# A decoder layer on one core: some operand sums moved from VectorE to GpSimd, two filler products in each of the first four slots, and the fillers of the last slots kept to one set of PSUM banks

## The chip, the core and the metric

The kernel runs on one core of a Trainium2 chip. The engines go by the names of the profile: PE is TensorE (matmuls), DVE is VectorE, ACT is ScalarE, POOL is GpSimd, SP issues DMAs. The metric is device time in microseconds (us) of one execution. Three runs of the kernel before gave 655.74, 656.04 and 656.16 us: the median is 656.04.

## What is computed

The layer has an input x of 2 batches × 512 tokens × 1024 features, all in float32:

```python
x = x + attention(layernorm(x))      # 32 heads of 32, 8 key/value heads, RoPE, causal
x = x + xattn(layernorm(x), ctx)     # both sides fake-quantised to 0..255, then a 1024x1024 matmul
x = x + ffn(layernorm(x))            # x @ W_org.T + LoRA experts (8 x rank 64), mixed by a softmax
                                     # over the mean token's scores
fake_quant(v) = (clip(round(v / s + z), 0, 255) - z) * s
```

The projections to queries, keys and values have 1536 output columns: 1024 for queries, 256 for keys, 256 for values.

## The kernel before

**Projections by seven products.** A projection of one weight column (a pair of 128-wide blocks; six columns in the order k, 0, 1, v, 2, 3) is a 2 × 2 block product: two halves of the features, and the two batches. It is computed with seven products of sums instead of eight, after Strassen's scheme. One product (`quarter`, L748) is four matmul calls of 128 × 512, each of which shows as two records, so "x8" in a group of records is one product. The products need sums of their operands, which are made in place:

- of the weights of a column c, T1 to T4 (`weight_sums`, L858), each one subtraction of 128 × 512: T1 = low − other_low, T2 = other_high − T1 (in its own tile t2), T3 = other_low := other_high − other_low, T4 = high − T2. All four are on DVE, one after the other in the lane `(1, "T")`. T2 of a column waits until product P6 of the column two before it is done, since they share a tile.
- of x, S3, S2, S1 and S4 (`sums_of_x`, L885), each in four pieces of 128 × 512, on DVE, in the lane `(0, "S")`. S2 lies in a tile named oT; S4 is a12 − S2 and overwrites a12, so it waits until the product that reads the old a12 (of the last first-stage item, `("first", 2)`) is done.

`g_second` (L787) makes, for each column, P6 from S2 and T2 (records "bank<-oT,t"), P5 from S1 and T1, and P3 from S4; `g_third` (L813) makes P7 with T3 and P4 with T4. Every product is added from PSUM into its result by DVE (L743).

**Slots.** Attention goes through 40 slots, `visit(i)` (L2040). Slot i makes four score tiles on PE (L1120) into the four banks of one set of PSUM. DVE takes a row minimum of each (L1132) and ACT the exponentials and their totals (L1147). When a group of slots is complete, ACT takes logarithms and POOL turns the totals into small terms (nine small operations, L1193 to L1201); a DMA transposes them to mT. Four slots later (LAG = 4) the scores are made again the other way round, together with these terms ("weights", L1218 and L1226), ACT takes their exponentials into pt (L1240), POOL masks the diagonal tiles (L1245), and PE multiplies them by v (L1267). So there are 44 visits, the last four without new scores.

**Fillers.** PSUM has eight banks, two sets of four. Two sets change places with each slot: in each visit the new scores go to one and the weights of LAG slots earlier to the other. Between slots, `fill(us)` gives PE other work: the products of the projections at first, then, for batch 0, the output projection (wo), the quantised matmul (q2, q1T) and others. `fill` adds `us` to a credit (RATE_1 = 5.0 us for slots before 24, RATE_2 = 3.6 after) and takes units from a queue while the credit is over half of UNIT = 3.44 us. A filler's bank comes from the list `allowed`: the four banks of the set `new`, or in the last LAG visits of `1 - new`. In the first four slots, where no weights are made, the fills take 1, 2, 1 and 2 products.

**Who sets the order.** The engines run their instructions in the order in which the program was written. A planner (`Clocks`, L119) models each engine's time and a duration for every instruction. Work beside PE stands in lanes of "hops", each with its engine, its inputs and a condition; `dispatch` (L529) writes hops whose inputs are ready by the model, lanes in sorted order. `force` writes a hop at once when the next unit must have it.

**The quantised matmul.** Row sums of the quantised context are needed for a correction: `g_columns` (L1384) multiplies them by a matrix of ones into bank "cs" (one for each half of 512 columns). For batch 0 this is a sum of eight matmuls per half over the eight tiles q2. For batch 1, in the part after the attention, POOL first adds the eight tiles (q2sum, L1377 to L1382, seven additions of 128 × 1024 in f16), and the matmul takes the sum (L1390). `chain_units` (L1890) says what this unit depends on.

After the slots come the products of the rest: the output projection of batch 1, the feed-forward matrix ("worg"), hidden and up of the experts (L1774, L1821, L1857), with the same scheme of seven products, and sums on DVE.

Of the kernel before, what the change touches and what calls it, by code (L numbers as in the profile page):

```python
# [13 lines left out]
ALU = mybir.AluOpType  # L14
AX = mybir.AxisListType

P = 128
# [30 lines left out]

RATE_1, RATE_2 = 5.0, 3.6
EARLY = 24  # L50
# [61 lines left out]
class Clocks:  # L112
# [45 lines left out]
    def add(self, ins):  # L158
# [48 lines left out]
        else:  # L207
# [8 lines left out]
            elif engine == "Pool":  # L216
                us = 0.25 + 0.0008 * many
            elif kind == "CustomDveAnt":
                us = 0.08 + 0.00104 * many
            elif kind == "TensorScalarPtr" and len(ins_) < 2 + 2 and not ins.is_scalar_tensor_tensor:  # L220
                us = 0.12 + 0.00058 * many
            else:
                us = 0.08 + 0.00106 * many
                if kind == "TensorScalarPtr":
                    us += 0.05
                elif kind == "TensorTensor" and self.at["Pool"] > start and not _in_psum(ins_):
                    us += 0.1
# [19 lines left out]
def kernel(  # L247
# [250 lines left out]
    lanes = {}  # L498
    LEAD = 0.6
    LEADS = {"Activation": 5.0, "Pool": 5.0}  # L500

# [113 lines left out]
    def any_may():  # L615
        return any(may_start(key) for key, _ in queue)

    def fill(us):

        credit[0] += us  # L620
        while any_may() and (is_open() or credit[0] > UNIT / 2):
            if not step():
                credit[0] = min(credit[0], UNIT)
                break

# [232 lines left out]
    def weight_sums(c):  # L858
# [5 lines left out]
        def second():  # L864
# [4 lines left out]
            minus_(t2[c], other_high, low)  # L869

        def fourth():
            minus_(high, high, t2[c])

        may = lambda: xn_free[0] > 0 if i == 0 else i == 1 or ("P6", COLUMNS[i - 2]) in done
        lane(
            (1, "T"),
            Hop("DVE", lambda: minus_(low, other_low, low), lambda: [low, other_low], key=("T", c, 1)),
            Hop("DVE", second, lambda: [other_high], may, ("T", c, 2), lambda: [t2[c]]),
            Hop("DVE", lambda: minus_(other_low, other_high, other_low), key=("T", c, 3)),
            Hop("DVE", fourth, key=("T", c, 4)),  # L880
        )
# [3 lines left out]
    def sums_of_x():  # L885
# [6 lines left out]
        def pieces(i, fn, can=None):  # L892
# [11 lines left out]
        )  # L904
        pieces(
            4,
            lambda k: minus_(a12[:, k, :], a12[:, k, :], s2[:, k, :]),
            lambda: ("first", 2) in done,
        )

# [376 lines left out]
    def load_ctx(b, bufs, dst, release):  # L1287
# [72 lines left out]
        if free[0]:  # L1360
            for k in range(1, CTX // P):
                mine = [("q2", b, i) for i, (n_, _) in enumerate(parts) if n_ in (k - 1, k)]
                last = {"key": ("q2sum", b), "made": lambda: [q2sum[b]]} if k == CTX // P - 1 else {}
                lane(
# [19 lines left out]
    def g_columns(b):  # L1384
        corr[b] = const.tile([P, D], F32, tag="corr", name=f"corr{b}")
        for h in range(2):
            cols = slice(h * 512, (h + 1) * 512)
            ps = mm([P, 512], f"cs{b}_{h}")
            if b in q2sum:
                nc.tensor.matmul(ps, onesh, q2sum[b][:, cols], start=True, stop=True)  # L1390
                yield 0.22
# [498 lines left out]
    def chain_units(b, w_keys):  # L1890

        turned = [("q", n) for n in range(B * NC)] + [("k", n, h) for n in range(B) for h in range(2)]
        columns = [("q2sum", b)] if b else [("q2", b, i) for i in range(CTX // P)]
        unit(("cs", b), turned + columns, lambda: g_columns(b))
# [145 lines left out]
    def visit(i):  # L2040
# [20 lines left out]
        hold(max(when_free))  # L2061
        empty([(old, s) for s in range(4)])
        sc, st = sets[new], sets[old]
# [6 lines left out]
        for s in range(4):  # L2070
            if s == 1 and g >= 0:
                empty([(new, 0)])
                pv = take_bank((new, 0))
                attend(g, pv)
# [13 lines left out]
        if g >= 0:  # L2088
            attended_to(g, pv)
        filler[0] = new  # L2090
        last_slots = i + 1 >= n_slots
        allowed[:] = [(1 - new if last_slots else new, s) for s in range(4)]
        dispatch()
        fill(RATE_1 if i < EARLY else RATE_2)
        if finishing is not None:
# [222 lines left out]
```

## Time and profile before

| | |
|---|---|
| median of three runs | 656.04 us |
| profiled execution | 655.19 us |
| its span | 653.5 us |
| PE busy | 631.9 us (97%) |
| DVE busy | 514.5 us (79%) |
| ACT busy | 299.6 us (46%) |
| POOL busy | 128.8 us (20%) |
| granted PE clock | 0.999 of full |

The span is the time from the first to the last instruction in the profile; 1.7 us of the execution lie around it. In a timeline, a line gives start, duration, engine, the source line, the operation and "output<-inputs" by the program's names, and in brackets how long the engine was idle before it and what ended that. In the waits, a line says which group waited for which, the total in us, how many times, and the longest. In a table of windows, each engine has its busy time and number of instructions, followed by the granted clock, the DMA share and GB/s.

### The profile page before, as it was taken

How to read it: one execution, taken by the hardware profiler on the slowest of the kernel's cores; microseconds unless marked ns; L12 is line 12 of the kernel's file. 1: busy time of each engine (PE TensorE's matmuls, PEld its weight loads, DVE VectorE, ACT ScalarE, POOL GpSimd, SP SyncE). 2: the span in 40 equal slices, each digit the busy share in tenths (PEclk: the TensorE clock that was granted, in tenths of full speed). 3: DMA queues.
4: the chain of work that ended last, by engine and by line, in shares of the span. 5: the costliest groups of instructions: out<-in, count | busy, mean ns of one | idle time of the engine just before them, and what ended most of it. 6: DMA issues, size and time to landing. Idle time of an engine off the chain costs nothing. (4 is left out here: it accounts for less than half of the span.)

```text
span 653.5 us, 9247 instructions
## 1 busy us (share of the span) xinstructions
PE 631.9 (97%) x3190; PEld 301.6 (46%) x3190; DVE 514.5 (79%) x1187; ACT 299.6 (46%) x808; POOL 128.8 (20%) x253
## 2 busy tenths in 40 slices
PE   5998999999999999999999999999999999999997
PEld 5753344444444444444444444444345544444443
DVE  5799889888778988888887689998998544553685
ACT  2145576686655768888897433554101100110100
POOL 2100133233313232333233320440110000000000
PEclk9999999999999999999999999999999999999999
DMA  9930000002021230120101146591000002000105
GB/s 290 335 83 2 9 9 10 10 1 73 10 73 65 73 106 10 46 101 34 33 2 25 25 134 237 169 314 32 1 1 0 33 31 97 1 0 1 65 0 193
DMA packets 42478, 44.64 MB, mean 68 GB/s; under 512 B 19264, under 2 KB 32576, under 8 KB 42432
## 3 DMA queue, kind: packets, MB, share of 16 engines
q1 hardware_dynamic: 24992, 38.82, 17.4%
q10 hardware_dynamic: 17440, 5.25, 4.2%
q8 instruction: 25, 0.41, 0.2%
q14 instruction: 21, 0.17, 0.1%
HBM read 35.66 MB, written 4.19 MB: 61 GB/s over the span
## 5 line engine op out<-in xcount | busy, mean ns | idle before, releaser
L1147 ACT ACTIVATE ms<-ms,stats 128x512 f32<-128x512 f32 (+3 forms) x256 | 141.0, 558 | 70.1 <-DVE stats L1132 70.1
L1132 DVE CUSTOM_DVE_ANT_0 ms<-bank,mask 128x512 f32<-128x512 f32 (+3 forms) x256 | 108.5, 487 | 14.7 <-PE bank L1120 12.9
L1240 ACT ACTIVATE pt<-bank 128x512 f32<-128x512 f32 x160 | 88.0, 590 | 25.3 <-PE bank L1267 9.0
L751 PE MATMUL bank<-xT,wq 128*128 128x512 f32 x192 | 88.0, 600 | 2.7 <-DVE stats L1132 2.7
L1245 POOL TENSOR_SCALAR_AFFINE_SELECT pt<-pt 128x512 f32<-128x512 f32 x64 | 48.9, 782 | 94.5 <-ACT pt L1240 90.3
L1411 PE MATMUL bank<-wo,oT 128*128 128x512 f32 x128 | 59.1, 604 | 0.7 <-ACT pt L1240 0.7
L751 PEld LDWEIGHTS bank<-xT,wq 128*128 128x128 f32 x192 | 34.7, 190 | 41.3 <-issue 35.7
L1218 PE MATMUL bank<-qT,kT 32*128 32x128 f32 (+3 forms) x512 | 49.3, 439 | 1.3 <-DVE x L1420 0.6
L1147 ACT ACTIVATION_READ_ACCUMULATOR ms<-ms,stats 128x1 f32 x256 | 50.1, 196 | 0.0
L1120 PE MATMUL bank<-kT,qT 32*128 32x128 f32 (+3 forms) x512 | 49.0, 461 | 0.0
L1120 PEld LDWEIGHTS bank<-kT,qT 32*128 32x128 f32 x512 | 24.2, 183 | 34.9 <-ACT pt L1240 10.5
L1267 PE MATMUL bank<-pt,v 128*32 128x128 f32 (+3 forms) x512 | 37.8, 435 | 0.0
L1411 PEld LDWEIGHTS bank<-wo,oT 128*128 128x128 f32 x128 | 23.1, 189 | 26.8 <-issue 24.2
L1193 POOL TENSOR_TENSOR stats<-stats,log 128x16 f32<-128x16 f32 x16 | 6.5, 409 | 142.7 <-ACT log L1184 100.3
L1218 PEld LDWEIGHTS bank<-qT,kT 32*128 32x128 f32 x512 | 25.6, 185 | 14.6 <-issue 7.8
L1795 DVE TENSOR_TENSOR x<-x,bank 128x512 f32<-128x512 f32 x36 | 23.1, 680 | 11.1 <-PE bank L1774 5.7
L1411 PE MATMUL bank<-q,q1T 128*128 128x512 bf16 x128 | 28.6, 379 | 1.6 <-ACT pt L1240 1.6
L1267 PEld LDWEIGHTS bank<-pt,v 128*32 128x32 f32 x512 | 16.4, 109 | 27.7 <-issue 24.8
L1774 PE MATMUL bank<-worg,S 128*128 128x512 f32 x64 | 28.3, 592 | 0.0
L1774 PE MATMUL bank<-worg,x3T 128*128 128x512 f32 x64 | 28.0, 594 | 0.0
L1774 PE MATMUL bank<-tb,S 128*128 128x512 f32 x64 | 27.9, 593 | 0.0
L743 DVE TENSOR_TENSOR qT<-bank,qT 128x512 f32<-128x512 f32 x28 | 18.9, 686 | 9.6 <-PE bank L751 9.5
(226 smaller groups left out, 1021.4 us busy)
## 6 DMA issues: line engine op xcount, KB each, us to landing
wq<-in_wqT_dram SPq DMA_DIRECT2D x8, 512.0 KB, 8.5
ctx_raw<-in_ctx_dram SPq DMA_DIRECT2D x8, 512.0 KB, 3.2
wo<-in_woT_dram SPq DMA_DIRECT2D x8, 512.0 KB, 3.1
raw<-in_ctx_dram SPq DMA_DIRECT2D x8, 512.0 KB, 3.9
worg<-in_worgT_dram SPq DMA_DIRECT2D x8, 512.0 KB, 6.2
out_dram<-x SPq DMA_DIRECT2D x16, 256.0 KB, 2.1
x<-in_x_dram SPq DMA_DIRECT2D x7, 512.0 KB, 6.7
x_raw<-in_x_dram SPq DMA_DIRECT2D x4, 512.0 KB, 7.4
```

The costliest lines, as they stand in the source:

```text
L743: nc.vector.tensor_tensor(dst, ps, other, ALU.add)
L751: nc.tensor.matmul(ps[:, part], weight[:, k, :], xs_[:, k, part], start=(k == 0), stop=(k == n - 1),)
L1120: nc.tensor.matmul(sc[s][:, part], qTs[b, c][row(s), t * P : (t + 1) * P], kTs[b][row(s), c // 4, : (t + 1) * P], start=True, stop=True,)
L1132: nc.vector.tensor_tensor_reduce(out=of[s][:, part], in0=sc[s][:, part], in1=mask[:, S - (t + 1) * P :], scale=-scale, scalar=BIG, op0=ALU ...
L1147: nc.scalar.activation(ms[:, part], ms[:, part], AF.Exp, bias=stats[g][:, t, s, 0:1], scale=-1.0, accum_out=stats[g][:, t, s, 1:2],)
L1218: nc.tensor.matmul(sc[s][:, part], kTs[b][row(s), c // 4, kb * P : (kb + 1) * P], qTs[b, c][row(s), kb * P :], start=True, stop=False,)
L1240: nc.scalar.activation(pt[:, s, :], sc[s][:, :n], AF.Exp, scale=scale)
L1245: nc.gpsimd.affine_select(out=diagonal, in_=diagonal, compare_op=ALU.is_ge, fill=0.0, base=0, pattern=[[0, 4], [1, P]], channel_multiplier=-1,
L1267: nc.tensor.matmul(pv[row(s), kb * P :], vs[b][:, kb, h * HD : (h + 1) * HD], pt[:, s, part], start=(kb == 0), stop=(kb == NT - 1),)
L1411: nc.tensor.matmul(ps, l[:, t * P : (t + 1) * P], r[:, cols], start=(k == 0), stop=(k == many - 1))
L1774: nc.tensor.matmul(ps[i], l[:, k, i * P : (i + 1) * P], r(k), start=(k == 0), stop=(k == n - 1))
L1795: nc.vector.tensor_tensor(xh, xh, src, ALU.add)
```

## The change

- T3 and T4 of each column go from DVE to POOL (GpSimd), in a lane of their own, `(1, "T34")`; T1 and T2 stay. T2 of a column now also waits for T4 of the column two before it.
- S4's four pieces go from DVE to POOL, in a lane `(1, "S4")`.
- In the first four slots a fill tops the credit up to two units, and `allowed` holds both sets; once less than one and a half units of credit are left, it is cut back to the set `filler[0]`. Visits up to LAG empty both sets.
- `filler[0]` is changed only in slots with new scores, and `allowed` is the set `1 - new` only after the last of these. So in the last four visits the weights go to the same set each time, and the fillers and the attention product (now from `mm`) to the other.
- POOL adds seven instead of eight tiles into q2sum (six additions); the eighth goes into the bank by a second matmul of each half. The unit's dependences for batch 1 are all q2 tiles and q2sum.
- RATE_1 is 4.7 instead of 5.0, the planner's duration of a two-input operation on POOL is 0.1 + 0.0021 n us, and a fill that finds no step to make calls `dispatch` with a lead of 2.5 us.

```diff
-RATE_1, RATE_2 = 5.0, 3.6
+RATE_1, RATE_2 = 4.7, 3.6
...
-                us = 0.25 + 0.0008 * many
+                us = 0.1 + 0.0021 * many if kind == "TensorTensor" else 0.25 + 0.0008 * many
...
         while any_may() and (is_open() or credit[0] > UNIT / 2):
+            if len(allowed) > 4 and credit[0] < 1.5 * UNIT and not is_open():
+                allowed[:] = [p for p in allowed if p[0] == filler[0]]
             if not step():
                 credit[0] = min(credit[0], UNIT)
+                dispatch(IDLE)
                 break
...
+        def third():
+            nc.gpsimd.tensor_tensor(other_low, other_high, other_low, ALU.subtract)
+
         def fourth():
-            minus_(high, high, t2[c])
-
-        may = lambda: xn_free[0] > 0 if i == 0 else i == 1 or ("P6", COLUMNS[i - 2]) in done
+            nc.gpsimd.tensor_tensor(high, high, t2[c], ALU.subtract)
+
+        def may():
+            if i < 2:
+                return i == 1 or xn_free[0] > 0
+            return ("P6", COLUMNS[i - 2]) in done and ("T", COLUMNS[i - 2], 4) in done
+
         lane(
             (1, "T"),
             Hop("DVE", lambda: minus_(low, other_low, low), lambda: [low, other_low], key=("T", c, 1)),
             Hop("DVE", second, lambda: [other_high], may, ("T", c, 2), lambda: [t2[c]]),
-            Hop("DVE", lambda: minus_(other_low, other_high, other_low), key=("T", c, 3)),
-            Hop("DVE", fourth, key=("T", c, 4)),
+        )
+        lane(
+            (1, "T34"),
+            Hop("Pool", third, tuple, lambda: ("T", c, 1) in done, key=("T", c, 3)),
+            Hop("Pool", fourth, lambda: [t2[c]], lambda: ("T", c, 2) in done, key=("T", c, 4)),
         )
...
-        pieces(
-            4,
-            lambda k: minus_(a12[:, k, :], a12[:, k, :], s2[:, k, :]),
-            lambda: ("first", 2) in done,
-        )
+        for k in range(n):
+            last = {"key": ("S", 4)} if k == n - 1 else {}
+            lane(
+                (1, "S4"),
+                Hop(
+                    "Pool",
+                    lambda k=k: nc.gpsimd.tensor_tensor(a12[:, k, :], a12[:, k, :], s2[:, k, :], ALU.subtract),
+                    tuple,
+                    lambda: ("first", 2) in done and ("S", 2) in done,
+                    **last,
+                ),
+            )
...
-            for k in range(1, CTX // P):
+            for k in range(1, CTX // P - 1):
                 mine = [("q2", b, i) for i, (n_, _) in enumerate(parts) if n_ in (k - 1, k)]
-                last = {"key": ("q2sum", b), "made": lambda: [q2sum[b]]} if k == CTX // P - 1 else {}
+                last = {"key": ("q2sum", b), "made": lambda: [q2sum[b]]} if k == CTX // P - 2 else {}
...
             if b in q2sum:
-                nc.tensor.matmul(ps, onesh, q2sum[b][:, cols], start=True, stop=True)
+                nc.tensor.matmul(ps, onesh, q2sum[b][:, cols], start=True, stop=False)
+                yield 0.22
+                nc.tensor.matmul(
+                    ps, onesb, q2_of(b, CTX // P - 1)[:, cols], start=False, stop=True
+                )
                 yield 0.22
...
-        columns = [("q2sum", b)] if b else [("q2", b, i) for i in range(CTX // P)]
+        columns = [("q2", b, i) for i in range(CTX // P)] + ([("q2sum", b)] if b else [])
...
-        empty([(old, s) for s in range(4)])
+        empty([(old, s) for s in range(4)] + [(new, s) for s in range(4) if i <= LAG])
...
             if s == 1 and g >= 0:
-                empty([(new, 0)])
-                pv = take_bank((new, 0))
+                pv = take_bank((new, 0)) if i < n_slots else mm([P, S], f"pv{g}")
...
-        filler[0] = new
-        last_slots = i + 1 >= n_slots
-        allowed[:] = [(1 - new if last_slots else new, s) for s in range(4)]
+        if i < n_slots:
+            filler[0] = new
+        allowed[:] = [(1 - new if i + 1 == n_slots else new, s) for s in range(4)]
+        if i < LAG:
+            allowed.extend((old, s) for s in range(4))
         dispatch()
-        fill(RATE_1 if i < EARLY else RATE_2)
+        fill(2 * UNIT - credit[0] if i < LAG else RATE_1 if i < EARLY else RATE_2)
```

More of the change, by code (lines that the diff above doesn't have):

```diff
@@ L499 @@
     LEAD = 0.6
+    IDLE = 2.5
     LEADS = {"Activation": 5.0, "Pool": 5.0}
```

## The prediction

> **What bounds the kernel now.** First the shares: PE is busy 631.9 of 653.5 us (97%) at a granted clock of 0.999, DVE 79%, ACT 46%, POOL 20%. So the end is set by how much PE work there is and by PE's gaps, and the gaps are few enough to be listed. The waits of the PE engine, which sum the idle time in front of its groups by what ended it, come second:
>
> ```profile
> PE bank L473 <- DVE xn_a L465: 7.3, 1, 7.3
> PE bank L751 <- DVE stats L1132: 3.6, 4, 1.0
> PE bank L1411 <- ACT pt L1240: 2.3, 3, 0.9
> PE bank L1390 <- POOL q2sum L1382: 1.3, 1, 1.3
> PE bank L473 <- ACT pt L1240: 0.8, 1, 0.8
> ```
>
> The first line is the start of the kernel. The other four, 3.57 + 2.27 + 1.26 + 0.80 = 7.90 us, are places the diff touches. The timeline of PE shows the late ones; the first two lines are of slots 2 and 3, the last of the second context correction:
>
> ```profile
> 62.67 3.70 PE L751 MATMUL bank<-xT,wq 128*128 128x512 f32 x8 [0.96 <-DVE stats L1132]
> 68.32 3.70 PE L751 MATMUL bank<-oT,t 128*128 128x512 f32 x8 [0.88 <-DVE stats L1132]
> ...
> 358.01 1.89 PE L1411 MATMUL bank<-q,q1T 128*128 128x512 bf16 x8 [0.71 <-ACT pt L1240]
> 360.79 1.89 PE L1411 MATMUL bank<-q,q1T 128*128 128x512 bf16 x8 [0.89 <-ACT pt L1240]
> 364.64 3.70 PE L1411 MATMUL bank<-wo,oT 128*128 128x512 f32 x8 [0.67 <-ACT pt L1240]
> 378.51 1.14 PE L473 MATMUL bank<-ident,xn_c 128*128 128x128 f32 x8 [0.80 <-ACT pt L1240]
> ...
> 467.67 0.59 PE L1390 MATMUL bank<-q2sum,onesh 128*128 128x512 f16 x2 [1.26 <-POOL q2sum L1382]
> ```
>
> In each of the first four slots the filler product goes to a PSUM bank whose scores DVE is still reading for their minima (0.77, 0.96, 0.96 and 0.88 us). In the last four slots fillers go to the set that ACT's exponentials still read. At 467.67 two matmuls wait for the last of seven adds on POOL. Third, the windows by stage (PE, PEld, DVE, ACT, POOL busy):
>
> ```profile
> 45.80:77.00 31.20, 27.63 (x121) 11.92 (x124) 27.45 (x76) 15.69 (x52) 2.62 (x9) 1.00 0.02 5
> 77.00:130.00 53.00, 52.90 (x342) 24.38 (x335) 46.93 (x136) 37.50 (x115) 16.68 (x36) 1.00 0.04 9
> 355.00:385.00 30.00, 26.93 (x207) 12.48 (x209) 20.29 (x37) 14.26 (x31) 11.75 (x21) 1.00 0.11 21
> 385.00:467.00 82.00, 81.41 (x224) 36.88 (x213) 77.55 (x127) 32.44 (x36) 19.46 (x12) 1.00 0.55 174
> ```
>
> In 45.8 to 77 us PE and DVE are equally full; POOL is nearly empty there. From 77 to 130 PE has no gap, with DVE at 89%. From 385 to 467 DVE is at 95% while PE has hardly a gap.
>
> **The change, part by part.** A product here is four matmul calls, eight records of 0.429 us from start to start: 3.43 us.
>
> *1. Two products in each of the first four slots.* Slots 0 to 3 took 1, 2, 1, 2 products, now 2, 2, 2, 2; both PSUM sets are allowed, and the first product of a slot goes to the old set, whose readers are done. PE's amount of work does not change, and the 3.57 us of waits on minima go. What is late next: products come earlier, so their operands are asked for earlier. Slot 2's first product is now P6(k), whose x operand S2 is made on DVE in four pieces of 128x512. The order on DVE puts two pieces ahead of slot 2's minima and two behind:
>
> ```profile
> 61.83 0.42 DVE L1132 CUSTOM_DVE_ANT_0 ms<-bank,mask 128x256 f32<-128x256 f32 x1 [0.47 <-PE bank L1120]
> 64.59 0.69 DVE L644 TENSOR_TENSOR oT<-xT,xT 128x512 f32<-128x512 f32 x1
> ```
>
> These minima take 61.83 to 64.59, 2.76 us. In the changed kernel PE reaches the scores of slot 2 at 60.56 (old start) − 1.73 (two waits gone) + 3.43 (one product more) = 62.26, P6(k) at 62.9, its third piece at 62.9 + 4 × 0.43 = 64.6. DVE begins the minima near 63.2, ends them at 65.95, and the third piece is there at 66.6: a new stall of 2.0 us. It is 0 if DVE takes the pieces ahead of the minima, which the written order excludes, and 3.0 if the minima start a microsecond later. I take 2.0. The fourth piece (67.2) and P5(k)'s operand S1 (a piece each 0.62 us against 0.86 us of matmul) add nothing.
>
> *2. S4 on GpSimd (four subtractions of 128x512, f32).* The trace has no such operation on POOL. The nearest rows are q2sum's 128x1024 additions: 2117 ns at best, 2260 median, 2932 at worst. Half of 2.12 is 1.06 us; below it stands DVE's 0.62 us for the same shape, above it the whole 2.12. I take 1.06, as cost per element is what the rows suggest. The four stand behind slot 2's statistics chain (nine small operations, 3.2 us alone, 4.2 to 4.5 when held up), so from about 70.9: ends at 72.0, 73.05, 74.1, 75.2, while the product that reads them wants 72.8, 73.7, 74.5, 75.4. Price 0 to 0.5 (with 2.12 each: 4), I take 0.2.
>
> The GPSIMD Engine Reference of the Trainium skill (4.1 Engine selection) speaks against this part: two-input elementwise work belongs on VectorE, GpSimd takes about twice as long. By its table for 2048 elements an estimate for one piece is 1.12 us, which makes the last piece 0.25 us later and the sum as much worse; no row of this trace has that shape on POOL.
>
> *3. T3 and T4 of six columns on GpSimd (12 × 128x512).* DVE is freed of 16 × 0.62 = 10 us together with S4, POOL gains 16 × 1.06 = 17 us in the first 130 us, where it has 19 of 84 us busy: room enough. The price is contention, which rows of the last stage show:
>
> ```profile
> 426.83 2.12 POOL L1382 TENSOR_TENSOR q2sum<-q2sum,q 128x1024 f16<-128x1024 f16 x1
> 427.40 1.57 DVE L1440 TENSOR_TENSOR off_b<-off_b,qp_sb 128x1 f32<-128x1 f32 x1
> ```
>
> A DVE operation on one element a row, 0.16 us elsewhere (426.64), takes 1.57 us and ends with POOL's. The same holds for S<-x3T at 436.15 (2.28 us, 1.21 at 464.10). DVE operations with a PSUM operand keep 0.67 to 0.69 us in all twelve overlaps I found, so minima and product additions are not held themselves, only queued behind one that is. Slot 4 is the tight place: its weights need the addition of P6(0), which stands on DVE behind T1 and T2 of column 1, each of which may sit out one POOL operation. Bounds 0.1 and 1.2 us, I take 0.5. In slots 5 to 12 and in the last stage's adds the slack is 0.4 to 0.8 us against holds of up to 1.06: 0 if all hide; 5 if five reach PE; I take 0.6, since PE showed no gap from 77 to 130 although rope operations there already alternate with POOL's selects (one at 89.79 is held from 0.75 to 1.20 us).
>
> The Trainium skill's page SBUF — State Buffer (section SBUF: two separate sides) calls the pair of ports shared by GpSimd and Vector an exclusive lock for a whole instruction, which blocks the other fully. If every POOL sum held DVE for its whole length, the 17 us would cancel the 10 us freed and leave DVE 7 us more; the rows above agree on the blocking, but show it only where DVE's two inputs are both in SBUF.
>
> *4. Last slots keep to the empty set.* Fillers of the last four slots go to the set without exponentials: 3.07 us of waits go. But all weights now go to one set: those of slots 37 and 38 must wait for ACT to read those before. Between the weights of 36 and 37 lie two products, between 37 and 38 only eight transposes (0.87 us) against four exponentials of 0.59 us. Bounds: 0 and 2.36 for the first, 0 and 2.36 − 0.87 = 1.5 for the second. I take 0.7 (the exponentials there start late, behind POOL's selects and the DMA that turns the terms, 2.4 us) and 1.1; for slot 39 nothing, as the last attention product (2.36 us) lies between. Sum 1.8.
>
> *5. q2sum with six adds.* The last tile goes into PE itself: the 1.26 us goes, and two matmuls of 0.215 us come (+0.43). The correction also comes one product (3.43 us) later, so POOL's sixth add, a tile earlier, is covered several times; the wait that takes its place is ACT's last q (ends 465.4), which has 4.4 us of slack. Cost beyond 0.43: nothing, or up to 1.3 if that slack is spent by DVE's 95%.
>
> *6. The rest.* RATE_1, the planner's POOL price and IDLE change only the order written out. From slot 13 to the first context correction PE's order is the same; one SP DMA less is issued and three are reordered, all of rows asked for microseconds ahead (3.1 to 6.2 us to landing, DMA 55% at most): 0.
>
> **Sum.** Off: 3.57 + 3.07 + 1.26 = 7.90. On: 2.0 + 0.2 + 0.5 + 0.6 + 1.8 + 0.43 = 5.53. Net −2.4: the profiled execution's 655.19 becomes 652.8. The median of the runs shown is 0.85 above that execution, so I forecast 653.6.
>
> **Rivals.** (A) The new stalls hide: ACT and DVE shift with PE and only the extra matmuls remain: −7.9 + 0.43 = −7.5, 648.6. For it: POOL is idle in 45.8 to 77; against it: S2's place in DVE's order. (B) Stalls swapped one for one: the dearer values of 1 to 4 with the matmuls (3.0 + 0.5 + 1.2 + 0.8 + 2.0 + 0.43) make 7.9: 656, within 0.2%. (C) Slower: POOL's lock. POOL's 16 sums hold DVE's two-input sums and rope operations, product additions queue behind, and the weights or scores of slots 4 to 12 wait. It decides from 2.4 us more on PE than my 1.1, two or three holds in full; 0.9 us in five more places gives 4.5 − 2.4 = +2.1 on the median, 658.1. For it: DVE 89% there; against: DVE has 10 us less to do. (D) The late rule does not deliver, as the weights pay the fillers' wait in full (2.36 + 1.5 for 3.07): +2.1 on my sum, 655.7.
>
> **How the numbers follow.** Runs of this kernel differ by 0.06%, and 0.2%, 1.3 us, is about what can be told from no change. Forecast 0.45, A 0.14, B and D together 0.19, C 0.22. Faster by over 1.3 us (below 654.7): forecast and A, 0.59; same: B and D, 0.19; slower: C, 0.22. The forecast's own range is 651 to 655; the range for 8 in 10 takes in most of A and the nearer half of C: 649.0 to 658.0.
>
> **What would show it.** Right: no PE wait on the minima in the first four slots; one wait of about 2 us near 64.6 of the product from oT and t on DVE's oT; POOL sums of 1.0 to 1.2 us; waits of the weights on exponentials of about 0.7 and 1.1; no wait on q2sum. Wrong if the POOL sums take 2 us, if PE waits on DVE additions between 77 and 130, or if the tail after 385 gets gaps that it did not have.

## The result, and the profile after

The changed kernel takes 666.75 us, median of five runs (666.42 to 667.26). The kernel before took 656.04 in five runs beside it (655.74 to 658.12). The ratio is 1.0159, with an interval of 1.0143 to 1.0176: slower by 10.7 us where 2.4 us faster was forecast. The profiled execution took 667.26 us with a span of 665.5, against 655.19 and 653.5. So the profile has 12.0 us more to explain.

The waits of PE in the kernel after (which group waited for what, total us, times, longest):

```profile
PE bank L1436 <- DMA q1T<-a_b: 5.3, 1, 5.3
PE bank L755 <- DVE oT L648: 1.7, 1, 1.7
PE bank L1239 <- DVE qT L747: 1.2, 3, 0.6
...
PE bank L1799 <- DVE tb L648: 0.8, 1, 0.8
PE bank L1411 <- POOL q2sum L1403: 0.7, 1, 0.7
```

The waits on the minima (3.57 us) and on the exponentials in front of fillers (3.07 us) are gone, as the change says. The wait of 1.7 us on oT is the forecast one. The line at the top is new: one wait of 5.3 us for a DMA, in a place that the prediction costed at nothing. PE's timeline there, in the kernel after:

```profile
385.77 3.70 PE L1799 MATMUL bank<-wo,oT 128*128 128x512 f32 x8
389.53 3.40 PE L1436 MATMUL bank<-q,q1T 128*128 128x512 bf16 x15
398.24 5.31 PE L1436 MATMUL bank<-q,q1T 128*128 128x512 bf16 x16 [5.31 <-DMA q1T<-a_b]
```

Two things are to be seen. PE has nothing from 392.9 to 398.24. And the second group, with one record more, takes 5.31 us where the first took 3.40. The windows of the kernel after say why (PE, PEld, DVE, ACT, POOL busy; granted clock; DMA share; GB/s):

```profile
386.00:398.00 12.00, 6.87 (x23) 2.78 (x23) 9.63 (x15) 3.18 (x5) 0.55 (x1) 1.00 0.96 300
398.00:401.00 3.00, 2.76 (x7) 1.02 (x8) 0.00 (x0) 0.94 (x1) 0.00 (x0) 0.55 0.30 116
401.00:404.00 3.00, 3.00 (x12) 1.46 (x11) 1.16 (x2) 0.00 (x0) 0.00 (x0) 0.88 0.13 31
```

After the gap the granted clock is 0.55 for three microseconds and 0.88 for the next three: the lost clock costs 3 × 0.45 + 3 × 0.12 = 1.7 us on top of the gap. From 386 to 398 us the 16 DMA engines are 96% busy, so the transfer that PE waits for is not held by an idle queue: other transfers run beside it. What was issued around it, on the SP and ACT queues and on DVE, in the kernel after:

```profile
386.02 1.75 SPq L320 DMA_DIRECT2D x<-in_x_dram  x4
...
386.97 0.69 DVE L1487 TENSOR_SCALAR a_b<-xn_b 128x1024 bf16<-128x1024 f32 x1
...
387.71 1.39 ACTq L1535 DMA_TRANSPOSE q1T<-a_b  x1
387.82 1.27 SPq L1317 DMA_DIRECT2D raw<-in_ctx_dram  x2
```

And the same in the kernel before:

```profile
381.72 1.00 DVE L1462 TENSOR_SCALAR a_b<-xn_b 128x1024 bf16<-128x1024 f32 x1
...
382.76 1.25 ACTq L1510 DMA_TRANSPOSE q1T<-a_b  x1
...
385.65 2.06 SPq L320 DMA_DIRECT2D x<-in_x_dram  x4
```

Before, the DMA that transposes the last quantised row tile (a_b to q1T) was issued 2.9 us ahead of four loads of x, 512 KB each. Now it is issued 1.7 us behind them, because a_b is made at 386.97 instead of 381.72, while PE runs only 0.4 us later at this place (the product of wo starts at 385.77 instead of 385.40). The view of the tile q1T gives the time from issue to landing, first in the kernel before, then in the kernel after:

```profile
DMA to landing us min/median/max: 3.1/3.1/6.4
```

```profile
L1436 PE MATMUL bank<-q,q1T x124: 379/379/634, 334.2 to 502.0; 128*128 128x512 bf16 x124
...
DMA to landing us min/median/max: 3.0/3.1/10.5
```

387.71 + 10.5 = 398.2 is the moment at which PE starts again. (In the first line, 634 ns against a median of 379 is a matmul at the lowered clock.) The 6.4 of the kernel before is another of the eight; its last one before the loads took 3.1.

The Trainium skill's page "DMA: Bandwidth & Descriptors" (section Issuing engines are not separate DMA queues) says that DMAs started by different engines run on the same 16 DMA engines and interleave. This case agrees and gives it a size: 3.1 us for the transposing DMA by itself, 10.5 us beside the 2 MB of x and 1 MB of context that SP had issued around it.

The second new place is slot 12. PE's timeline of the kernel after:

```profile
151.17 2.61 PE L1141 MATMUL bank<-kT,qT 32*128 32x512 f32 x6
154.12 0.69 PE L1141 MATMUL bank<-kT,qT 32*128 32x512 f32 x1 [0.35 <-ACT pt L1261]
```

Scores that take 1.14 us elsewhere are spread over 3.5 us here (the second line is their seventh record of eight, the eighth starts at 154.65) and go bank by bank behind ACT's exponentials. No filler product stands between the weights and the scores of the next slot. The fillers that the program wrote between the scores of one slot and the next, in us by the planner's durations, slot by slot:

```
slot     0   1   2   3   4   5   6   7   8   9  10  11  12   13
before 3.4 6.9 3.4 6.9 6.9 3.4 3.4 6.9 3.4 6.9 3.4 3.9 6.9  3.4
after  6.9 6.9 6.9 6.9 6.9 3.4 3.4 3.4 6.9 3.4 3.9 6.9 0.0 10.3
```

The first four slots take two products more, the following ones use up theirs earlier, and by slot 12 the queue has reached a column whose unit needs two new q tiles (the buffers for query results) while 11 of the 12 are still in use. Nothing may start there; it comes a slot later.

### The profile page after: what moved, and what is told of

Read it like the earlier page. It is cut to its first block, busy times and chain, and to the rows that moved or that the text cites. A ratio compares the mean times of both kernels' runs of the same rounds, so it can differ in the third digit from the quotient of the medians.

```text
span 665.5 us, 9260 instructions
## 1 busy us (share of the span) xinstructions
PE 642.3 (97%) x3186; PEld 305.7 (46%) x3192; DVE 512.5 (77%) x1173; ACT 299.4 (45%) x806; POOL 144.9 (22%) x268
## 4 chain that ended last, share of the span: by engine, by line
PE 78%; DVE 13%; issue 3%; ACT 2%; DMA 2%; POOL 1%; ACTq 0%; SPq 0%; DVEq 0%; POOLq 0%
PE bank L755 20%; PE bank L1799 12%; PE bank L1436 10%; PE bank L1882 7%; PE bank L1846 7%; PE bank L1141 6%; PE bank L1239 5%; PE bank L1288 5%; PE bank L473 2%; DVE ms L1153 2%; DMA q1T<-a_b 2%; PE bank L1247 1%; DVE x L1820 1%; DVE S L648 1%; DVE x L1067 1%
## 5 line engine op out<-in xcount | busy, mean ns | idle before, releaser
L1153 DVE CUSTOM_DVE_ANT_0 ms<-bank,mask 128x512 f32<-128x512 f32 (+3 forms) x256 | 108.4, 486 | 16.8 <-PE bank L1141 13.7
L1266 POOL TENSOR_SCALAR_AFFINE_SELECT pt<-pt 128x512 f32<-128x512 f32 x64 | 47.5, 759 | 76.7 <-ACT pt L1261 73.3
L1239 PE MATMUL bank<-qT,kT 32*128 32x384 f32 (+3 forms) x512 | 56.4, 439 | 2.2 <-DVE qT L747 1.2
L1141 PE MATMUL bank<-kT,qT 32*128 32x128 f32 (+3 forms) x512 | 52.3, 460 | 0.3 <-ACT pt L1261 0.3
L1239 PEld LDWEIGHTS bank<-qT,kT 32*128 32x128 f32 x512 | 29.4, 185 | 16.1 <-issue 6.0
L1436 PE MATMUL bank<-q,q1T 128*128 128x512 bf16 x124 | 30.1, 396 | 5.5 <-DMA q1T<-a_b 5.3
```

The source lines that it names most:

```text
L1141: nc.tensor.matmul(sc[s][:, part], qTs[b, c][row(s), t * P : (t + 1) * P], kTs[b][row(s), c // 4, : (t + 1) * P], start=True, stop=True,)
L1153: nc.vector.tensor_tensor_reduce(out=of[s][:, part], in0=sc[s][:, part], in1=mask[:, S - (t + 1) * P :], scale=-scale, scalar=BIG, op0=ALU ...
L1239: nc.tensor.matmul(sc[s][:, part], kTs[b][row(s), c // 4, kb * P : (kb + 1) * P], qTs[b, c][row(s), kb * P :], start=True, stop=False,)
L1266: nc.gpsimd.affine_select(out=diagonal, in_=diagonal, compare_op=ALU.is_ge, fill=0.0, base=0, pattern=[[0, 4], [1, P]], channel_multiplier=-1,
L1436: nc.tensor.matmul(ps, l[:, t * P : (t + 1) * P], r[:, cols], start=(k == 0), stop=(k == many - 1))
```

## The experiments

Theory A: the loss lies in the written order, at two places that the engines' loads do not show: the DMA near 386 us, which the late rule moved behind the loads, and the empty slot 12. Theory B, the rival C of the prediction: the sums on GpSimd hold VectorE, and PE waits for what queues behind them.

**1. The x loads issued behind the last transposing DMA, in the kernel after.** No instruction of PE, DVE or POOL moves.

```diff
+    force(("A", 0, NT - 1))
     for t in range(NT):
         xi = tail_x([P, D], f"x1_{t}")
-        load_x(xi, NT + t)
+        nc.scalar.dma_start(xi, x[(NT + t) * P : (NT + t + 1) * P, :])
```

> The changed kernel, with one thing moved: the four loads of batch 1's x (2 MB) are issued on ACT's queue right behind the transposing DMA of the last quantised row tile (q1T of tile 3), instead of on SP's queue 1.7 us ahead of it. No instruction of PE, DVE or POOL changes its place. Theory A (collision): the 5.31 us wait of PE at 398.24 is that DMA held to 10.5 us by the loads ahead of it; with 3.1 to 4.5 us it lands before PE asks for it at 392.9, so the 5.3 us go, and with them the 1.5 us that the lowered clock costs behind the gap: 666.75 - 6.8 = 660.0. Theory B (POOL holds DVE, and the loss is in the slots): the wait at 398 is only where lateness from the slots is collected; the time stays at 666 to 667, with the lateness showing at another place.

Measured: 659.82 us (658.94 to 660.44, seven runs), ratio to the kernel before 1.0049 [1.0033, 1.0065]. That is 6.9 us less than the kernel after. The issues on ACT's queue, and the tile's DMA:

```profile
387.90 1.25 ACTq L1535 DMA_TRANSPOSE q1T<-a_b  x1
...
389.24 2.30 ACTq L2171 DMA_DIRECT2D x<-in_x_dram  x4
```

```profile
L1436 PE MATMUL bank<-q,q1T x124: 379/379/389, 334.4 to 494.7; 128*128 128x512 bf16 x124
...
DMA to landing us min/median/max: 3.1/3.1/4.1
```

The transposing DMA starts as late as in the kernel after, but lands in 4.1 us at most, PE does not wait, and no matmul is slow. The wait and the lowered clock, 5.3 + 1.7 = 7.0 us, are the loads' doing.

**2. The late rule undone in the kernel after.**

```diff
-                pv = take_bank((new, 0)) if i < n_slots else mm([P, S], f"pv{g}")
+                empty([(new, 0)])
+                pv = take_bank((new, 0))
...
-        if i < n_slots:
-            filler[0] = new
-        allowed[:] = [(1 - new if i + 1 == n_slots else new, s) for s in range(4)]
+        filler[0] = new
+        last_slots = i + 1 >= n_slots
+        allowed[:] = [(1 - new if last_slots else new, s) for s in range(4)]
```

> The changed kernel, with the rule of the last slots as it was before (the sets change places in the last four visits too, fillers in the set that the exponentials read, the attention product in a bank of its own). Theory A with the late rule as its cause: the order of the last slots is again that of before, the quantising of the last row tile is written ahead of the x loads, and the 6.8 us go, while the four waits on exponentials (3.1 us) take the place of the two waits of the weights (2.3): 666.75 - 6.8 + 0.8 = 660.7. Theory B: nothing that matters is in the last slots, 666 to 668. If the late rule is not what moved the quantising, the wait at 398 stays and the time is 667 to 668.

Measured: 660.92 us (660.69 to 663.46, five runs), 1.0074 [1.0049, 1.0099]. No wait on the DMA (it lands in 3.7 us at most, and is issued at 388.97, ahead of the loads at 391.91). The waits that the late rule had removed are back:

```profile
PE bank L1436 <- ACT pt L1261: 1.9, 2, 1.7
...
PE bank L1799 <- ACT pt L1261: 0.8, 1, 0.8
PE bank L473 <- ACT pt L1261: 0.7, 1, 0.7
```

So it is the late rule that put the DMA behind the loads. It loses 7.0 us there to take away 3.4.

**3. The sums back on VectorE in the kernel after (T3, T4 and S4).** These parts of the change's diff are taken out, and all else stays.

> The changed kernel, with T3, T4 and S4 back on DVE (and the planner's price of GpSimd operations as before). Theory A: the wait at 398 stays if it comes from the late rule; of the rest, the holds of DVE by POOL (1.3 us at slot 9 near 122, 0.6 at slot 4, 0.3 at slot 8) go: 666.75 - 2.2 = 664.5. Theory B: most of the 10.7 us goes, 656 to 658.

Measured: 678.63 us (676.49 to 679.22, four runs), 1.0329 [1.0298, 1.036]. Neither theory had this: 12 us slower than the kernel after, where B said faster. Its waits:

```profile
PE bank L1419 <- DMA q1T<-a_b: 5.5, 1, 5.5
PE bank L1394 <- POOL q2sum L1386: 4.2, 1, 4.2
PE bank L755 <- DVE xT L648: 2.3, 1, 2.3
```

The DMA wait is there as before. S4, back on DVE, comes 2.3 us too late for the two products of slot 3. The correction waits 4.2 us for POOL at a place that the sums do not touch: in the written order one product of worg (3.5 us) stands ahead of it, where the kernel after has two. The clock is the largest item: a mean of 0.985 over 677.0 us lacks 10.2 us of clock, where the kernel after (0.997 of 665.5) lacks about 2. Theory B falls as the account of the loss, since the time does not come back with the sums on DVE. How much the sums alone are worth this run does not say, as most of its 12 us lie in places that they do not touch.

**4. The first slots filled by `RATE_1` again, in the kernel after** (and only one set allowed). As RATE_1 is 4.7 here, the fills take 1, 2, 1 and 1 products, one fewer than in the kernel before.

> The changed kernel, with the fills of the first four slots as before (1, 2, 1, 2 products, new set only). In the changed kernel the stretch 46 to 82 us loses as much time on PE as before (4.5 against 4.2 us): the four waits on minima are replaced by 1.72 us for S2 and 0.6 at slot 4. So undoing it alone is worth between 0 and +1.5 by the stretch itself: 666.5 to 668, if the tail keeps its order. If the tail's order turns on how many products have been made by slot 36, the wait at 398 goes here too: 660 to 661.

Measured: 663.52 us (662.43 to 664.69, four runs), 1.0104 [1.0069, 1.0138]. The waits of PE:

```profile
PE bank L1237 <- ACT pt L1259: 5.8, 2, 3.1
PE bank L753 <- DVE stats L1151: 4.8, 4, 2.0
```

The waits on the minima return, larger than before (as in experiment 6), and slot 12 is filled. But the fillers now run out at the other end: slots 39 and 40 get none, and the weights wait 5.8 us for ACT from 355 us on. The DMA comes early enough here. The first slots have fewer products than in the kernel before, and yet the stock ends earlier: by the written order a product goes ahead of the scores of nearly every slot from 14 on, beyond the credit (`hold`). So this run does not give the price of the two early products alone; experiment 8 does, in the kernel before.

**5. Slot 12 filled, on top of experiment 1.** One product goes from slot 11 to slot 12.

```diff
-        fill(2 * UNIT - credit[0] if i < LAG else RATE_1 if i < EARLY else RATE_2)
+        goal = 2 * UNIT if i < LAG else {11: UNIT, 13: 8.72}.get(i)
+        fill(goal - credit[0] if goal else RATE_1 if i < EARLY else RATE_2)
```

> The kernel of the first experiment (the changed kernel with the x loads behind the transposing DMA), with the fills of two slots set by hand: slot 11 takes one product instead of two, slot 12 one instead of none, slot 13 three as it did. In the changed kernel no product may start after slot 11, since two products run ahead and 11 of 12 q tiles are in use (the next column needs two), so the scores of slot 13 follow the attention product at 151 us directly and wait for ACT at each bank (2.0 us), and the weights behind them lose about 1 us. Theory A (running ahead of the q tiles): 659.8 - 2.0 to 3.0 = 656.8 to 657.8. Rival (those scores wait for ACT, which is late by itself): the wait moves to the next slot, 659 to 660.

Measured: 656.49 us (655.94 to 657.48, ten runs), 1.0003 [0.9992, 1.0013]: 3.3 us less than experiment 1, and the same as the kernel before. PE's timeline where the stall was:

```profile
146.49 3.70 PE L755 MATMUL bank<-xT,wq 128*128 128x512 f32 x8
150.12 1.14 PE L1141 MATMUL bank<-kT,qT 32*128 32x512 f32 x8
```

The scores take 1.14 us again. The two places of theory A together are 10.2 of the 10.7 us.

**6. The sums on GpSimd alone, in the kernel before.**

> The kernel before, with T3, T4 and S4 on GpSimd alone (and the planner's price for them). The sums took 1.26 to 2.18 us each in the changed kernel's profile, not 1.06. Theory B (POOL holds DVE, DVE's queue holds PE): holds of 0.3 to 1.3 us at two or three of the slots 4 to 12, 656 + 2 = 657 to 659. Rival (DVE is relieved of 10 us, and the holds are hidden, as the products come no earlier here): 655 to 656.5.

Measured: 659.51 us (658.23 to 661.51, six runs), 1.0048 [1.0028, 1.0068]. Slower alone: the first wait on the minima grows from 0.77 to 2.0 us (all four: 4.8 instead of 3.6), the weights wait 1.1 us for kT, and in the profiled execution the clock drops for 3.4 us behind the first wait (from 49.3 us). That first wait is theory B at work: T1 and T2 of a column take 1.77 and 1.64 us at 42.09 and 43.89, beside POOL's sums of 41.52 to 46.65, where each takes 0.69 in the kernel before, and the minima behind them begin at 48.66 instead of 47.00. The drop of the clock is not needed for the loss: the three of six executions with a mean clock of 0.999 or 1.0 took 658.2 to 658.7 us.

**7. The late rule alone, in the kernel before.**

> The kernel before, with the rule of the last slots alone. If the rule by itself moves the last quantising behind the x loads, the wait for the transposing DMA comes with it: 656 - 3.1 + 2.3 + 6.8 = 662. If it takes the rule together with the two products that were made earlier (which shift what is left to fill in the last slots), there is no such wait: 656 - 3.1 + 2.3 = 655.2.

Measured: 668.23 us (666.4 to 668.35, four runs), 1.0171 [1.0146, 1.0195]. The one edit costs as much as the whole change:

```profile
PE bank L1390 <- POOL q2sum L1382: 6.1, 1, 6.1
PE bank L1411 <- DMA q1T<-a_b: 4.9, 1, 4.9
```

The transposing DMA is issued at 383.36 us here, 0.1 us *ahead* of the loads of x, and still lands only after 8.9 us. The wait of 6.1 us is new: DVE's rounding of the last two raw tiles is written late, so two POOL additions run one after the other (4.9 us from 473.23) with PE waiting.

**8. Two products in the first slots alone, in the kernel before.**

> The kernel before, with two products in each of the first four slots alone. By the written order slots 12, 40, 41 and 42 get no filler at all, as the products run out of q tiles at 12 and of ready work at the end. Off: 3.57 us of waits on minima. On: 1.7 for S2, 2.3 for S4 behind S1 on DVE, 2 to 3 for slot 12, and in the last three slots the weights wait for the exponentials of the set that they have just filled, 4 to 8 us: 656 + 6 to 11 = 662 to 667. Rival (the fills only change places): 653 to 656.

Measured: 664.57 us (663.27 to 666.16, four runs), 1.0125 [1.01, 1.0149]. Waits of 1.7 us on oT and 2.3 us on xT (S4, still on DVE), the latter with half the clock for 3.4 us behind it, the empty slot 12 (its scores start at 152.89, their last record at 156.38) with half the clock for 6.8 us behind it, and empty slots at the end.

**9. Half of S2 on GpSimd, on top of experiment 5.** The stall of 1.7 us on oT is S2's third piece.

```diff
-        pieces(2, lambda k: minus_(s2[:, k, :], a22[:, k, :], a11[:, k, :]))
+        lane((0, "S"), Hop("DVE", lambda: minus_(s2[:, 0, :], a22[:, 0, :], a11[:, 0, :])))
+        lane((0, "S"), Hop("DVE", lambda: minus_(s2[:, 1, :], a22[:, 1, :], a11[:, 1, :]), key=("S", "2a")))
+        for k in (2, 3):
+            fn = lambda k=k: nc.gpsimd.tensor_tensor(s2[:, k, :], a22[:, k, :], a11[:, k, :], ALU.subtract)
+            lane((0, "S2p"), Hop("Pool", fn, tuple, lambda: ("S", "2a") in done, key=("S", 2) if k == 3 else None))
```

> The kernel of the fifth experiment, with the last two of S2's four pieces on GpSimd instead of DVE, behind DVE's first two. POOL is idle from 47 to 66 us there. The stall of 1.72 us in P6(k) comes, by the prediction's step 1, from those two pieces standing on DVE behind slot 2's minima (they end at 65.60, the third piece at 66.3, PE wants it at 64.6). On POOL they need about 1.27 us each from 61.7, beside minima that read PSUM and aren't held: ready at 63.1 and 64.4. Theory: the 1.72 us go, of which up to 0.3 come back in P5(k), as S1's pieces still follow the minima: 656.5 - 1.5 = 655.0. Rival (DVE is the bound of the stretch from 46 to 82 us, and the wait only moves to the next product or to slot 3's scores): 656.0 to 656.8.

Measured: 657.49 us (656.89 to 657.86, twelve runs), 1.0012 [0.9998, 1.0026]: no gain.

```profile
PE bank L755 <- DVE xT L919: 1.1, 1, 1.1
PE bank L755 <- POOL xT L929: 0.9, 2, 0.6
```

The 1.7 us is gone, and S1 (1.1) and S4 (0.9) wait in its place.

**10. The six additions alone, in the kernel before** (the two matmuls for each half, POOL one tile less).

> The kernel before, with q2sum of seven tiles and the eighth multiplied into the bank by PE, alone. The prediction's step 5: 1.26 us of wait go, 0.43 us of matmul come, 656.0 - 0.8 = 655.2. Rival (the wait is not POOL's last add but the clamp of the last tile on DVE, which is written late, at 463.5, and ACT's rounding behind it, 465.4: PE then waits for the seventh tile's add or for ACT): a wait of 0 to 0.7 stays, 655.2 to 656.2.

Measured: 654.25 us (653.82 to 655.2, twelve runs), 0.9963 [0.9949, 0.9977]. It is the only part that gains, and faster than both kernels. Its timeline at the correction:

```profile
466.52 0.38 PE L1390 MATMUL bank<-q2sum,onesh 128*128 128x512 f16 x1
466.74 0.38 PE L1392 MATMUL bank<-q,onesb 128*128 128x512 bf16 x1
```

No wait stands in front of it. The spans of the two profiles differ by 0.7 us (652.8 and 653.5), the fastest runs by 1.4 (653.82 and 655.21), the ratio says 2.4; the runs of the kernel before reach up to 659.15 beside it. Part of the ratio is theirs: five of the 23 had a mean clock of 0.996 or 0.997 and took 658.15 to 659.15 us, the other 18 average 655.93, which is 1.6 us above the 654.32 of this run's twelve, all at 0.998 or more. The profile accounts for 0.7 us; where the other 0.9 come from stays open.

**11. The x loads later, on top of experiment 7** (the edit of experiment 1).

> The kernel of the seventh experiment (the kernel before with the late rule alone), with the four x loads issued on ACT's queue behind the last transposing DMA, as in the first. There the loads were issued 0.1 us after the transpose (383.46 against 383.36), not 1.7 us ahead of it, and it still took 8.9 us. If the loads' traffic is what holds it, the wait of 4.88 us and about 2.5 us of slower clock behind it go: 668.2 - 7.4 = 660.8. The wait of 6.13 us for q2sum (two of POOL's adds are written late, behind DVE's clamp at 471) and the slower clock behind it stay, as no order changes. Rival (the transpose is slow by itself at that place): 667 to 669.

Measured: 662.6 us (662.05 to 664.92, four runs), 1.0093 [1.0063, 1.0124]: 5.6 us less than experiment 7. PE still waits 3.6 us for q1T, which lands in 7.5 us: two loads of context (SP, 383.44) are issued 0.1 us behind it, and the x loads 1.4 us behind. In experiment 1, where the context was issued 1.7 us ahead and the x loads 1.3 us behind, it was 4.1. So 1 MB right behind the transposing DMA delays it, too. The 6.1 us on q2sum stays.

**12. Six additions, and both sets allowed in the first slots with the old fills** (1, 2, 1, 2), in the kernel before.

> The kernel before with the six adds of the tenth experiment, and with one rule of the changed kernel's first slots: where a fill of slots 0 to 3 has credit for two products (slots 1 and 3, as in the kernel before), the first goes to the old set, whose readers are done. The number of products in these slots stays 1, 2, 1, 2; all sums stay on DVE. Theory (the waits on the minima go, and the operands of P6 and P3 are asked for at most 1.8 us earlier, within what DVE has in hand): 654.3 - 0.96 - 0.88 = 652.4. Rival (DVE is the bound of 46 to 82 us, and each wait taken away there comes back at the next operand, as in the ninth experiment): 654.0 to 655.0.

Measured: 655.12 us (654.71 to 656.34, twelve runs), 0.998 [0.997, 0.9989]: not better than experiment 10.

```profile
PE bank L753 <- DVE stats L1134: 1.7, 2, 1.0
PE bank L1122 <- DVE qT L681: 1.5, 1, 1.5
...
PE bank L753 <- DVE xT L646: 0.6, 1, 0.6
```

Of the 3.6 us of waits on the minima 1.8 go; 1.5 on the queries and 0.6 on S4 come.

## Why the prediction was wrong

The step that failed is *6. The rest*: "RATE_1, the planner's POOL price and IDLE change only the order written out ... three are reordered, all of rows asked for microseconds ahead (3.1 to 6.2 us to landing, DMA 55% at most): 0." The largest price of the change was in the DMAs' order, and it came from the late rule, whose step (4) looked at PE and ACT alone. Three things should have stopped the zero. The landing times of up to 6.4 us against 3.1 showed that this DMA can be slowed (the 6.4 is the one issued at 431.48, beside loads of worg). The share of 55% was a mean over 82 us: from 385 to 400 us of the kernel before it is 1.01. And the last transposing DMA lay only 2.9 us ahead of the loads, so the chain that makes a_b on DVE had to be followed through the new order of the last slots. There the row tile before the last begins at 378.27 instead of 364.08, written behind a copy for which DVE waits 2.8 us for PE's attention product; the last one begins at 383.82 instead of 379.84, with 1.5 us of other work between its steps. Behind slot 4 a second term was left out: step 1 made products earlier and did not follow where they would then be missing (slot 12, below).

Against the profiled execution, term by term (us; the measured ones worked out from the two profiles and experiments 1 and 5):

| step | predicted | measured |
|---|---|---|
| start: scores of slot 0 at 46.54 instead of 45.84 | 0 | +0.7 |
| 1, 2: waits on the minima gone, S2 and S4 late | −3.57 + 2.0 + 0.2 = −1.4 | −1.7 |
| 3: slot 4 | +0.5 | +0.8 |
| 3: other holds, slots 5 to 12 | +0.6 | +1.3 |
| 4: late rule on PE and ACT | −3.07 + 1.8 = −1.3 | −0.9 |
| 5: six additions | −1.26 + 0.43 = −0.8 | −0.1 |
| slot 12 without filler, left out of step 1 | 0 | +3.3 |
| 6: last transposing DMA behind the loads, clock | 0 | +6.9 |
| weights at 350.77, not foreseen | 0 | +1.0 |
| sum | −2.4 | +11.3 of 12.0 |

The first row is not the change's: in four profiles whose order is the same up to there (the kernel after and experiments 1, 2 and 5) these scores begin between 45.29 and 46.72.

*Step 1* was right in its mechanism and its size. In the kernel after the product from oT and t goes from 63.89 to 69.41, 5.5 us instead of the 3.5 that one takes undisturbed, because of the wait forecast for "near 64.6 of the product from oT and t on DVE's oT" (1.72 us, at 67.59). By the scores of slot 4 (34.94 us after those of slot 0, instead of 29.54) PE has done two products more, worth 2 × 3.53: 1.7 us gained, for the 1.4 of steps 1 and 2. Two times of the working, 62.9 for P6(k) and 63.2 for the first minimum, are some 0.4 us early (a product starts 1.08 us after the scores ahead of it, 62.81 to 63.89 in the kernel after, and the first minimum 1.27 us after them, 60.56 to 61.83 in the kernel before); they cancel in the stall, which is luck. What it missed is behind slot 4: two products early are two fewer later, and slot 12 pays (experiments 5 and 8).

*Step 2:* S4 costs 0.4 (the product at 74.01 takes 3.94 us to the next) for 0.2.

*Step 3* took 1.06 us for a POOL sum. The groups of POOL in the kernel after:

```profile
L879 POOL TENSOR_TENSOR wq<-wq,t 128x512 f32<-128x512 f32 x4 | 6.0, 1498 | 1.4 <-DVE t L648 1.4
L876 POOL TENSOR_TENSOR wq<-wq 128x512 f32<-128x512 f32 x4 | 6.0, 1494 | 3.2 <-DVE wq L648 3.2
...
L925 POOL TENSOR_TENSOR xT<-xT,oT 128x512 f32<-128x512 f32 x4 | 5.0, 1271 | 0.0
```

They take 1.27 us where DVE is not in the way, and 1.50 on average beside it. The prediction's estimate of 1.12 us, worked out from the measured time for 2048 elements in the Trainium skill's "GPSIMD Engine Reference" (section 3.1 Elementwise — side-by-side cycle accounting), was nearer than half of a q2sum row, and still low. The hold works both ways: beside DVE POOL's sums are longer, and beside them DVE's operations are, which is rival C. DVE near slot 9 in the kernel after:

```profile
117.49 1.76 DVE L680 SCALAR_TENSOR_TENSOR qT<-qT,bqk_sb,trig 128x512 f32<-128x512 f32 x1
...
122.54 0.68 DVE L747 TENSOR_TENSOR v<-bank,v 128x512 f32<-128x512 f32 x1
```

A rope operation that takes 0.75 us alone takes 1.76 beside POOL's 116.97 to 118.70. The addition into v, queued behind, keeps its 0.68 us but comes late, and the weights behind it go from 122.03 to 124.55, 2.5 us for 1.2. At slot 4 it is T2 of a column, 1.79 us at 80.17 instead of 0.69, beside POOL's 80.15 to 81.42. So C's mechanism is there at 1.3 + 0.8 us, a fifth of the loss; it was given as the way in which the kernel could become slower, and it is not the way in which most of the loss came.

*Step 4:* "I take 0.7 ... and 1.1" for the weights; measured 1.1 and 1.1. The two groups in the kernel after, which go over several lines of the timeline because each matmul waits a little:

```profile
369.52 1.49 PE L1239 MATMUL bank<-qT,kT 32*128 32x256 f32 x7
...
372.84 1.82 PE L1239 MATMUL bank<-qT,kT 32*128 32x512 f32 x6
```

The second lasts from 372.84 to the attention product at 375.24, 2.40 us; before it was 368.27 to 369.56, 1.29. As a sum over PE and ACT the step was near; its place in the DMAs' order was left out. The weights at 350.77 lose 1.0 with the late rule undone as well (353.36 in experiment 2), so they are not the late rule's doing; which part of the change they belong to was not tried.

*Step 5* expected the wait on q2sum to be replaced by "ACT's last q ... 4.4 us of slack". Alone the step is right: the forecast was −0.8 and the span in experiment 10 is 0.7 shorter. In the changed kernel 0.7 us of the wait stays, since the sixth tile is not "a tile earlier". DVE, ACT and POOL in the kernel after:

```profile
478.73 1.29 DVE L1344 TENSOR_SCALAR raw<-raw 128x1024 f32<-128x1024 f32 x2
479.45 2.19 ACT L1348 ACTIVATE q<-raw,minus 128x1024 bf16<-128x1024 f32 x2 [11.62 <-DVE raw L1344]
480.74 2.39 POOL L1403 TENSOR_TENSOR q2sum<-q2sum,q 128x1024 f16<-128x1024 f16 x1 [22.62 <-ACT q L1348]
```

The last two tiles are rounded together at 478.73, after POOL has waited 22.6 us; the addition ends at 483.13, and PE's matmul starts at 483.19. The written order, again.

*The rivals.* A fell with the S2 stall. B's price of 7.9 us for the places that it named is near what they came to, 2.0 + 0.4 + 0.8 + 1.3 + 2.2 + 0.4 = 7.1, and without the two faults of order the change stands where B put it, at the time before (experiment 5). That it comes out so well is in part luck, as B has neither the 1.0 at 350.77 nor the 0.7 left on q2sum. D, the weights paying in full, did not happen: 2.2 us of 3.9. The sentence on what would make the forecast wrong named "if the tail after 385 gets gaps that it did not have": it did, by a DMA.

Two attempts to gain in the first 82 us got nothing: experiments 9 and 12 each take a named wait away (1.7, 1.8 us) and get as much back on other results of DVE and, in experiment 9, of POOL. That no order could gain there is not shown.

## What to carry to other kernels

Where a scheduler writes the order, a change of one rule moves DMAs too: list for every transfer that PE waits for soon what is issued within some 3 us ahead of it and behind it, and take the DMA share of that stretch, not of the stage. Where fillers are given out from a fixed stock, follow the stock to its end: the slot that will have none is the price of the slot that got more. And try the parts singly: here the one part that gained (0.9963 alone) was hidden under three that lost.

## What the runs showed that was not expected

**A gap can be paid twice.** In the kernel after the wait of 5.3 us is followed by half the clock for 3.4 us (398.3 to 401.7), 1.7 us of PE time. Each stretch of lowered clock behind a gap, in the profiles of the kernel after and of the experiments, is 3.4 us or a multiple: 3.4 us behind gaps of 2.04 us (experiment 6, at 49.3), of 2.26 us (experiments 3 and 8, at 77.1 and 78.0) and of 1.71 us (experiment 2, at 368.9), 6.8 us behind the empty slot 12 in experiments 2, 3 and 8, 13.7 us in experiment 4 (from 356.4). The length of the gap alone does not decide: the wait of 1.72 us on oT lowered the clock in none, and one of 2.04 us in experiment 4 (at 49.4) did not. The stall of slot 12 lowered it in experiments 2, 3 and 8, but not in the kernel after and in experiment 1, whose stall is the same. Nor does the kernel alone decide: of the five executions of experiment 2 the profiled one had a mean clock of 0.992 and took 663.46 us, the other four 0.999 or 1.0 and 660.69 to 661.10. What decides was not tried.

**A transposing DMA is slowed by loads, even by later ones.** It takes 3.1 us alone or 2.9 us ahead of the loads, 4.1 us with 1 MB issued 1.7 us ahead of it and 2 MB 1.3 us behind it, 7.5 us with 1 MB 0.1 us and 2 MB 1.4 us behind it, 8.9 us with 2 MB 0.1 us behind it, and 10.5 us with 2 MB 1.7 us ahead and 1 MB 0.1 us behind. To be first by 0.1 us was no protection; 1.3 us nearly sufficed. In what way the transfers share the engines these runs do not show.
